# Six exps per head group on VectorE with GpSimd's square, and the next group's q and keys loaded head by head, in a graph-attention kernel

## The chip, the cores and the metric

The kernel runs on one core of a Trainium2 chip, in one launch. The time is device microseconds; 10982.1 us is the median of three runs of the kernel before (10978.02 to 10984.69). Profiles are of one further execution each. The engines are called as in the profile: PE (TensorE), ACT (ScalarE), DVE (VectorE), POOL (GpSimd) and SP (SyncE, which here only issues DMAs).

## The reference

Four graph layers act on x, 3327 nodes by 128 features, with one dense 3327 x 3327 matrix `adj`. Each layer normalises x, applies its function and adds the result to x. The change concerns layer 0 alone, an attention with 128 heads of 8 elements, whose scores get `adj` added twice:

```python
q = (x @ Wq.T).reshape(d, n, h); k = ...; v = ...        # d = 128 heads, n = 3327, h = 8
a = jnp.einsum('dnh,dmh->dnm', q, k) * scale
a = a + spatial_encoding + edge_encoding                 # both are adj
a = jax.nn.softmax(a, axis=2)
out = jnp.einsum('dnm,dmh->dnh', a, v)
return out.reshape(n, h * d) @ Wo.T
```

So there are 128 x 3327 x 3327 exps. Layers 1 to 3 are multiplications with `adj` and hyperbolic maps; they take the last some 800 us and are not touched.

## The kernel before, in words

**Tiling.** Scores are made transposed, keys on the 128 partitions and queries along the free dimension. A *chunk* `c` is 476 queries (7 chunks), a *group* `g` is four heads (32 groups), and a *pair* `q` is two tiles of 128 keys (13 pairs, r = 0 and 1 for the two tiles). The loop runs over 7 x 32 x 13 = 2912 pairs `u`, chunk by chunk, group by group; there are 224 head groups. A pair owns two of seven PSUM banks of the tile `S`, one per key tile (`banks`, line 618), and keeps them for its four heads. When the two banks are neighbours, one ACT exp covers both (128 x 952); in one pair of seven they wrap around and take two exps of 128 x 476.

**One pair.** DVE *seeds* each bank with `adj` less a bound (`seed`, L645). PE adds head 0's scores; ACT takes exp(2 S) of the bank into the tile `e0` (`exps`, L666 for the double form, L669 for a single). For the next head PE adds the difference of the two heads' scores to the same bank (the tiles `QS` and `KT` hold the next q and the negated last one side by side), ACT takes the exp again into `e1`, and so on to `e3`. PE then multiplies the exps with the values, 9 columns per head, into the bank `po` (`values`, L713); at a group's last pair DVE copies `po` to `OS` (L721) and POOL issues four DMAs of it (L725).

**The exps by hand.** In the pairs of `BY_HAND` (0, 2, 5, 7 and 10 of each group, here called hand pairs) head 0's exp of the second key tile is not ACT's. Its bank starts without a seed; DVE reads the bare scores (L691, its result in `h`), seeds the bank, and evaluates a polynomial of degree four in three operations (L695) and one (L697) that also multiplies with `EA`, the exp of twice the seed, which `shifted` (L678) and `bare` (L683) make once per chunk and hand pair. So in a hand pair ACT's first exp is a single. Because the polynomial comes late, `heads_of` (L699) has PE take this exp into the values one turn later than the others.

**The order of the work is written out by hand.** One loop (line 796) runs over slots `i`, four per pair, each slot one ACT exp; a place such as "slot 2 of pair 3" means `i % 4 == 2` there. Head j of pair u has its exp in slot 4u + 3j, so heads of neighbouring pairs are interleaved. In each slot the instructions of every engine are issued in program order: the exp, the DVE steps of the polynomial (slot 0 of a hand pair: L691 and the bank's seed; slot 3: one operation; slot 0 of the next pair: two; its slot 3: the last), seeds in slot 1 (the next pair's second bank, unless that is a hand pair) and slot 2 (first bank of the pair after the next). In odd slots PE gets the scores of the next two slots and four heads' values of one tile. Engines run their queues in order and wait on semaphores.

**Loads.** `loads(u)`, at the end of slot 0, brings in the next group: at pair 1 all keys of its four heads (`load_k`, 16 DMAs of 104 or 208 KB), head 0's q (`load_q`, 6 DMAs, 9 for head 1) and the values `VR`; at pairs 3, 5 and 7 POOL writes the negated q of one head into `QS` (`negate_q`, L570) and SP loads the next head's q; at pair 8 POOL spreads the values into `VA` (L580) and copies one column of the keys into `seen` (`all_here`, L584), for which the next group's first scores wait. All of these go through SP's queue in program order. In some groups DVE also transposes squares of `adj` for the next chunk (L288).

Of the kernel before, what the change touches and what calls it, by code (L numbers as in the profile page):

```python
# [10 lines left out]
F32 = mybir.dt.float32  # L11
# [6 lines left out]
ALU = mybir.AluOpType  # L18
# [4 lines left out]
P = 128  # L23
N = 3327
D = 128
H = 8
# [3 lines left out]
NQ = NT // 2  # L30
# [6 lines left out]
CW = 476  # L37
# [8 lines left out]
NOTHING = -1.0e30  # L46


EXP_C = (0.9999990463256836, 2.2162604331970215, 2.4563632011413574, 1.8291265964508057)
EXP_ARG = 0.9023826718330383  # L50
BY_HAND = (0, 2, 5, 7, 10)
LN_EPS = 1e-5
L1_EPS = 1e-7
L1_MAX_TANH = 1.0 - 1e-6
# [34 lines left out]
def gnn_kernel(ctx: ExitStack, tc: tile.TileContext, x, adj, Wq, Wk, Wv, Wo, embed, layer,  # L89
               embed_bias, layer_bias, weight, bias, W_in, W_out, out):  # L90
    nc = tc.nc
# [14 lines left out]
    kS_d = dram.tile([2, H, HEADS, NP], F32, name="kS_d")  # L106
# [418 lines left out]
    with tc.tile_pool(name="e1", bufs=1) as e1, tc.tile_pool(name="e_adj", bufs=28) as e_adj, \  # L525
# [12 lines left out]
        S = e_ps.tile([P, 7, 512], F32, name="S")  # L538
        po = e_ps.tile([P, 512], F32, name="po")

        def load_k(c, g):

            b = (c * NG + g) % 2
            for j in range(4):
                d = 4 * g + j
                k0, nk = max(0, j - 1), 1 if j in (0, 3) else 2
                for r in range(2):
                    r0 = 64 * r + 32 * (1 - j % 2)
                    k_d = kS_d[:, :, d, r * NQ * P:(r + 1) * NQ * P].rearrange("i e n -> (i e) n")
                    for i in range(2):  # L550
                        nc.sync.dma_start(KT[b][r0 + 16 * i:r0 + 16 * i + 16, k0:k0 + nk, :].bitcast(F32),
                                          k_d.unsqueeze(1).to_broadcast([16, nk, NQ * P]))

        def load_q(c, g, j):

            b = (c * NG + g) % 2
            w, c0, d = width_of(c), c * CW, 4 * g + j
            q_d = qS_d[:, :, d * N + c0:d * N + c0 + w].rearrange("i e n -> (i e) n")
            for r in range(2):
                r0 = 64 * r + 32 * (1 - j % 2)  # L560
                for q_s in [QS[b][:, j, :]] + [QZ[b]] * ((r, j) == (1, 1)):
                    nc.sync.dma_start(q_s[r0:r0 + 16, :w].bitcast(F32), q_d)
                    for i in range(2):
                        nc.sync.dma_start(q_s[r0 + 16 + 8 * i:r0 + 24 + 8 * i, :w].bitcast(F32),
                                          q_d[8 - 8 * i:16 - 8 * i])
# [33 lines left out]
        with tc.If(loose < 1), tc.manual_schedule():  # L599
# [28 lines left out]
            def touch(u, rows, x):  # L628
                of = {banks(u)[r] for r in rows}
                for y, other in touched:  # L630
                    if not of & other and x.ins.engine != y.ins.engine:
                        tc.declare_no_dep(x.ins, y.ins, reason="other banks")
                for i in of:
                    if i in last:
                        tc.add_manual_dep(x.ins, last[i].ins.name, after, reason="the same bank")
                    last[i] = x
                touched.append((x, of))

            def bank(u, r):
                return S[:, banks(u)[r], :width_of(pairs[u][0])]  # L640
# [19 lines left out]

            def exps(u, j):
                w, (even, odd) = width_of(pairs[u][0]), banks(u)
                e = e_of[u, j] = e_e.tile([P, 2, CW], F32, name=f"e{j}", bufs=(5, 4, 3, 2)[j])
                hand = j == 0 and by_hand(u)
                if even > odd and not hand:
                    touch(u, (0, 1), nc.scalar.activation(e[:, :, :w], S[:, odd:even + 1, :w], AF.Exp, scale=2.0))  # L666
                    return
                for r in range(1 if hand else 2):
                    touch(u, [r], nc.scalar.activation(e[:, 1 - r, :w], bank(u, r), AF.Exp, scale=2.0))  # L669

            def by_hand(u):

                return 0 <= u < n and pairs[u][2] in BY_HAND

            def shifted(c, q):

                w = width_of(c)
                nc.vector.tensor_tensor(EA[q][:, :w], adj_of[c][2 * q + 1][:, :w], shift_of[c][:, :w], op=ALU.subtract)  # L678

            def bare(c, q):  # L680

# [3 lines left out]
            def hand_exp(u):  # L685


                w = width_of(pairs[u][0])
                s = e_h.tile([P, CW], F32, name="h")[:, :w]
                e = e_of[u, 0][:, 0, :w]  # L690
                touch(u, [1], nc.vector.tensor_scalar(s, bank(u, 1), EXP_ARG, None, op0=ALU.mult))  # L691
                seed(u, 1)
                yield
                for k in (3, 2, 1):
                    nc.vector.scalar_tensor_tensor(e, s if k == 3 else e, EXP_C[k], s, op0=ALU.add, op1=ALU.mult)  # L695
                    yield
                nc.vector.scalar_tensor_tensor(e, e, EXP_C[0], EA[pairs[u][2]][:, :w], op0=ALU.add, op1=ALU.mult)  # L697

            def heads_of(u, r):  # L699


                first = (u, r)
                if by_hand(u) and r == 1:
                    first = (u + 1, 0)
                elif by_hand(u - 1):
                    first = (u, 1) if r == 0 else (u - 1, 1)
                return [first] + [(u, r)] * 3

            def values(u, r):
                c, g, q = pairs[u]  # L710
                w, k = width_of(c), c * NG + g
                for j, (v, of) in enumerate(heads_of(u, r)):
                    nc.tensor.matmul(po[32 * j:32 * j + H + 1, :w], VA[k % 2][:, 2 * pairs[v][2] + of, j, :],  # L713
                                     e_of[v, j][:, 1 - of, :w], start=(q == 0 and r == 0),
                                     stop=(q == NQ - 1 and r == 1))

            def store(u):
# [9 lines left out]
            def loads(u):  # L727

                c, g, q = pairs[u]
                k = c * NG + g  # L730
                if k + 1 < NC * NG:
                    nxt = divmod(k + 1, NG)
                    if q == 1:
                        load_k(*nxt)
                        load_q(*nxt, 0)
                        v_of[k + 1] = load_v(*nxt)
                    if q in (3, 5, 7):
                        negate_q(*nxt, q // 2 - 1)
                        load_q(*nxt, q // 2)
                    if q == 8:  # L740
                        spread_v(*nxt, v_of.pop(k + 1))
                        here[k + 1] = all_here(*nxt)
                if c + 1 < NC and (g, q) == (0, 0):
                    plan_squares(c)
                if g == NG - 1 and c + 1 < NC:
                    if q == 0:
                        shift_of[c + 1] = load_shift(c + 1)
                        adj_of[c + 1] = []
                    while len(adj_of[c + 1]) < min(NT, 2 * q + 6):
                        adj_of[c + 1].append(load_adj(c + 1, len(adj_of[c + 1])))  # L750
# [17 lines left out]
                        plan(u + k, f)  # L768

            v0 = load_v(0, 0)  # L770
            load_k(0, 0)
            load_q(0, 0, 0)
            shift_of[0] = load_shift(0)
            for j in range(3):
                negate_q(0, 0, j)
# [20 lines left out]
            for i in range(-4, 4 * n + 15):  # L796
                u, j = in_slot(i)
                if 0 <= u < n:
                    exps(u, j)
                at = i % 4  # L800
                if i == -4:
                    seed(0, 0)
                if at == 0 and by_hand(i // 4):
                    by_vector.append(hand_exp(i // 4))
                    next(by_vector[-1])
                for k in range(0 if at % 3 else 1 if at else 0 if by_hand(i // 4) else 2):
                    if by_vector and next(by_vector[0], True):
                        by_vector.popleft()
                if at == 0 and i >= 0:
                    for f, a in behind.pop(i // 4, ()):  # L810
                        f(*a)
                if at == 1 and (i + 3) // 4 < n and not by_hand((i + 3) // 4):
                    seed((i + 3) // 4, 1)
                u = (i - 14) // 4
                if at == 2 and 0 <= u < n and pairs[u][2] == NQ - 1:
                    store(u)
                if at == 2 and (i + 6) // 4 < n:
                    seed((i + 6) // 4, 0)
                if at % 2:
                    for k in (1, 2):  # L820
                        u, j = in_slot(i + k)
                        if 0 <= u < n:
                            scores(u, j)
                    u, r = ((i - 11) // 4, 0) if at == 3 else ((i - 13) // 4, 1)
                    if 0 <= u < n:
                        values(u, r)
                if at == 0 and 0 <= i // 4 < n:
                    loads(i // 4)
# [678 lines left out]
```

## Time and profile before

| What | Value |
| --- | --- |
| Median of three runs | 10982.1 us |
| The profiled execution | 10981.96 us |
| Its span, first to last instruction | 10980.2 us |
| First and last exp of the attention loop (L666, L669) | 462.5 and 10167.6 us |
| Busy from 4000 to 6000 us: PE, ACT, DVE, POOL | 1982.40, 1995.56, 1606.90, 270.68 us |
| Granted TensorE clock from 1000 to 10000 us | 1.00 |
| DMA: share of 16 engines, rate from 4000 to 6000 us | 0.59, 97 GB/s |
| Instructions per whole run: L666, L669 | 9024, 4128 |
| L691, L695 (first of three), L695 (other two), L697 | 1120, 1120, 2240, 1120 |
| L645 (seeds), mean | 5824, 676 ns |

How to read the profile: a row of a timeline is the start (us), the time from the first start to the last end of the merged instructions, the engine, the line, output and inputs by tile names, shapes, a count, and in brackets the idle time before it and what ended it. A row of the groups has the count, then the busy time in all (us) and the mean of one (ns), then the engine's idle time before. Instructions of one engine overlap by their pipelines, so the step from start to start is what one costs in a full queue, and a mean duration is longer than that. An instruction that holds its engine while it waits counts as busy.

### The profile page before, as it was taken

To read this page: it belongs to the slowest core of one execution; us is meant where nothing else is said; L and a number is where in the kernel's file an instruction comes from. 1 tells how busy PE (TensorE), PEld (TensorE's weight loads), DVE (VectorE), ACT (ScalarE), POOL (GpSimd) and SP (SyncE) were. 2 spreads that over 40 slices of the span, in tenths; PEclk is the share of its full clock that TensorE was granted. 3 is DMA by queue.
4 is the path that set the end of the run, shared out by engine and by line. 5 is a ranking of instruction groups with operands and counts; after the bars stand their busy time and mean duration, and the time that the engine had idled before them with its cause. 6 is when DMAs were issued, how large, how long until landed. Compare 5 with 4: busy or idle time off the path is not lost. (4 is left out here: it accounts for less than half of the span.)

```text
span 10980.2 us, 204474 instructions
## 1 busy us (share of the span) xinstructions
PE 10533.5 (96%) x72876; PEld 3435.7 (31%) x72876; DVE 8487.1 (77%) x13503; ACT 10033.1 (91%) x13789; POOL 1529.1 (14%) x2477
## 2 busy tenths in 40 slices
PE   4599999999999999999999999999999999999889
PEld 2133333333333333333333333333323333333544
DVE  5588887888878887788887888878877777777655
ACT  3599999999999999999999999999999999999330
POOL 5011111111111111111111111111111111111101
PEclk7799999999999999999999999999999999999999
DMA  8766566565566565565556565565556555554668
GB/s 250 250 99 97 94 96 113 93 98 96 89 118 97 93 97 88 106 98 97 90 95 119 94 96 93 95 119 95 87 93 98 96 95 86 82 88 71 206 233 281
DMA packets 695339, 1256.98 MB, mean 114 GB/s; under 512 B 195218, under 2 KB 555049, under 8 KB 691244
## 3 DMA queue, kind: packets, MB, share of 16 engines
q1 hardware_dynamic: 644044, 1114.42, 55.7%
q0 software_dynamic: 50272, 129.37, 4.3%
q8 instruction: 587, 9.62, 0.4%
q14 instruction: 436, 3.57, 0.2%
HBM read 1096.53 MB, written 146.60 MB: 113 GB/s over the span
## 5 line engine op out<-in xcount | busy, mean ns | idle before, releaser
L666 ACT ACTIVATE e<-S 128x952 f32<-128x952 f32 (+1 forms) x9024 | 8357.9, 1099 | 36.7 <-PE S L654 29.4
L713 PE MATMUL po<-e,VA 128*9 128x476 f32 (+1 forms) x46592 | 5737.5, 564 | 33.0 <-DVE OS L721 12.3
L645 DVE TENSOR_TENSOR S<-a,shb 128x476 f32<-128x476 f32 (+1 forms) x5824 | 3937.9, 676 | 1447.6 <-ACT e L666 1059.4
L654 PE MATMUL S<-QS,KT 64*128 64x476 f32 (+1 forms) x22176 | 4528.6, 445 | 79.7 <-DMA a<-adjT 28.4
L654 PEld LDWEIGHTS S<-QS,KT 64*128 64x128 f32 x22176 | 2073.7, 184 | 5100.5 <-issue 1301.3
L669 ACT ACTIVATE e<-S 128x476 f32<-128x476 f32 (+1 forms) x4128 | 2467.5, 711 | 1.1 <-PE S L654 0.6
L695 DVE SCALAR_TENSOR_TENSOR e<-e,h 128x476 f32<-128x476 f32 (+1 forms) x2240 | 1497.8, 669 | 77.0
L713 PEld LDWEIGHTS po<-e,VA 128*9 128x9 f32 x46592 | 691.0, 88 | 1606.6 <-issue 1488.1
L570 POOL TENSOR_SCALAR QS<-QS 128x476 fp32r<-128x476 f32 (+1 forms) x672 | 485.6, 723 | 4312.1 <-DMA QS<-qS_d 2612.2
L725 POOL DMA_DIRECT2D oT_d<-OS x896 | 470.5, 530 | 3668.8 <-DVE OS L721 3625.5
L691 DVE TENSOR_SCALAR h<-S 128x476 f32<-128x476 f32 (+1 forms) x1120 | 728.0, 650 | 300.9 <-PE S L654 296.5
L697 DVE SCALAR_TENSOR_TENSOR e<-e,EA 128x476 f32<-128x476 f32 (+1 forms) x1120 | 759.6, 678 | 0.0
L695 DVE SCALAR_TENSOR_TENSOR e<-h 128x476 f32<-128x476 f32 (+1 forms) x1120 | 743.1, 663 | 0.0
L1107 PE MATMUL pu<-strip,y 128*128 128x512 f32 (+2 forms) x1456 | 600.5, 566 | 31.7 <-DVE y L968 14.8
L654 PE MATMUL S<-QZ,KT 64*128 64x476 f32 (+1 forms) x1120 | 493.4, 441 | 11.9 <-DVE S L645 10.5
L1107 PEld LDWEIGHTS pu<-strip,y 128*128 128x128 f32 (+1 forms) x1456 | 271.9, 191 | 305.8 <-issue 272.1
L1111 DVE TENSOR_REDUCE deg<-strip 128x1 f32<-128x1536 f32 (+1 forms) x104 | 193.8, 1881 | 63.7 <-DMA strip<-adjT 44.1
L580 POOL COPY VA<-VR 128x832 f32<-128x832 f32 x224 | 242.3, 1082 | 0.0
L654 PEld LDWEIGHTS S<-QZ,KT 64*128 64x128 f32 x1120 | 205.1, 183 | 92.2 <-DVE S L645 52.4
L288 DVE STREAM_TRANSPOSE cols<-rows 128x416 f32<-128x416 f32 x208 | 204.5, 988 | 30.3 <-DMA rows<-in_adj_dram 22.6
L1060 ACT COPY uT<-pu 128x512 f32<-128x512 f32 (+1 forms) x21 | 11.1, 555 | 222.6 <-PE pu L1107 222.6
L721 DVE COPY OS<-po 128x476 f32<-128x476 f32 (+1 forms) x224 | 146.3, 653 | 87.3 <-PE po L713 87.3
(255 smaller groups left out, 1958.6 us busy)
## 6 DMA issues: line engine op xcount, KB each, us to landing
KT<-kS_d SPq DMA_DIRECT2D x1792, 208.0 KB
KT<-kS_d SPq DMA_DIRECT2D x1792, 104.0 KB
VR<-v_d SPq DMA_DIRECT2D x224, 416.0 KB
QS<-qS_d SPq DMA_DIRECT2D x3072, 14.9 KB
QS<-qS_d SPq DMA_DIRECT2D x1536, 29.8 KB
adjT<-cols SPq DMA_DIRECT2D x26, 1664.0 KB
a<-adjT SPq DMA_DIRECT2D x156, 238.0 KB
strip<-adjT POOLq DMA_DIRECT2D x39, 895.5 KB, 5.1
```

The costliest lines, as they stand in the source:

```text
L570: nc.gpsimd.tensor_scalar(QS[b][:, j + 1, :w], QS[b][:, j, :w].bitcast(F32), -1.0, 0.0, op0=ALU.mult, op1=ALU.add)
L580: nc.gpsimd.tensor_copy(VA[(c * NG + g) % 2][:, :, :, 0:H], v.rearrange("p j (t e) -> p t j e", e=H))
L645: touch(u, [r], nc.vector.tensor_tensor(bank(u, r), adj_of[c][2 * q + r][:, :w], shift_of[c][:, :w], op=ALU.subtract))
L654: x = nc.tensor.matmul(bank(u, r), KT[b][64 * r:64 * r + 64, max(0, j - 1), q * P:(q + 1) * P], q_s[64 * r:64 * r + 64, :w], start=hand an ...
L666: touch(u, (0, 1), nc.scalar.activation(e[:, :, :w], S[:, odd:even + 1, :w], AF.Exp, scale=2.0))
L669: touch(u, [r], nc.scalar.activation(e[:, 1 - r, :w], bank(u, r), AF.Exp, scale=2.0))
L691: touch(u, [1], nc.vector.tensor_scalar(s, bank(u, 1), EXP_ARG, None, op0=ALU.mult))
L695: nc.vector.scalar_tensor_tensor(e, s if k == 3 else e, EXP_C[k], s, op0=ALU.add, op1=ALU.mult)
L697: nc.vector.scalar_tensor_tensor(e, e, EXP_C[0], EA[pairs[u][2]][:, :w], op0=ALU.add, op1=ALU.mult)
L713: nc.tensor.matmul(po[32 * j:32 * j + H + 1, :w], VA[k % 2][:, 2 * pairs[v][2] + of, j, :], e_of[v, j][:, 1 - of, :w], start=(q == 0 and r ...
L725: nc.gpsimd.dma_start(oT_d[:, d * N + c * CW:d * N + c * CW + w], o[32 * j:32 * j + H + 1, :w])
L1107: nc.tensor.matmul(ps[:, :k], y[:m, t, :], s[:m, c * 4 * P - c0:c * 4 * P - c0 + k], start=(t == 0), stop=(t == NT - 1))
```

## The change

1. `BY_HAND` is (0, 2, 4, 6, 8, 10): six exps per group by hand instead of five, always two pairs apart.
2. The polynomial of degree four is evaluated in another form: z = s + C0 (L691's place), z squared **by POOL**, then three DVE operations instead of four: z = (e + C1) + z with the square in e, e = (e + C2) * z, e = (e + C3) * EA. The leading factor goes into EA through `EXP_LEAD`.
3. The steps are moved: slot 0 of a hand pair has z, POOL's square and the seed; slot 0 of the next pair the first two of the three; its slot 3 the last operation. Slot 3 of a hand pair has none.
4. The values take all four heads in the same order everywhere (`heads_of` is gone), and `e0` has four buffers instead of five.
5. The next group's loads: at pairs 1, 3, 5 and 7 one head's q and then that head's keys; the values at pair 1; spreading and `all_here` at pair 9 instead of 8. The number and size of DMAs stay.

```diff
-BY_HAND = (0, 2, 5, 7, 10)
+BY_HAND = (0, 2, 4, 6, 8, 10)
...
-        def load_k(c, g):
+        def load_k(c, g, j):
...
-                e = e_of[u, j] = e_e.tile([P, 2, CW], F32, name=f"e{j}", bufs=(5, 4, 3, 2)[j])
+                e = e_of[u, j] = e_e.tile([P, 2, CW], F32, name=f"e{j}", bufs=(4, 4, 3, 2)[j])
...
-                nc.vector.tensor_tensor(EA[q][:, :w], adj_of[c][2 * q + 1][:, :w], shift_of[c][:, :w], op=ALU.subtract)
+                nc.vector.scalar_tensor_tensor(EA[q][:, :w], adj_of[c][2 * q + 1][:, :w], EXP_LEAD, shift_of[c][:, :w],
+                                               op0=ALU.add, op1=ALU.subtract)
...
-                s = e_h.tile([P, CW], F32, name="h")[:, :w]
+                v, add, mult = nc.vector.scalar_tensor_tensor, ALU.add, ALU.mult
+                z = e_h.tile([P, CW], F32, name="h")[:, :w]
                 e = e_of[u, 0][:, 0, :w]
-                touch(u, [1], nc.vector.tensor_scalar(s, bank(u, 1), EXP_ARG, None, op0=ALU.mult))
+                touch(u, [1], nc.vector.tensor_scalar(z, bank(u, 1), EXP_C[0], None, op0=add))
+                nc.gpsimd.tensor_tensor(e, z, z, op=mult)
                 seed(u, 1)
                 yield
-                for k in (3, 2, 1):
-                    nc.vector.scalar_tensor_tensor(e, s if k == 3 else e, EXP_C[k], s, op0=ALU.add, op1=ALU.mult)
-                    yield
-                nc.vector.scalar_tensor_tensor(e, e, EXP_C[0], EA[pairs[u][2]][:, :w], op0=ALU.add, op1=ALU.mult)
...
+                v(z, e, EXP_C[1], z, op0=add, op1=add)
+                yield
+                v(e, e, EXP_C[2], z, op0=add, op1=mult)
+                yield
+                v(e, e, EXP_C[3], EA[pairs[u][2]][:, :w], op0=add, op1=mult)
...
-                for j, (v, of) in enumerate(heads_of(u, r)):
-                    nc.tensor.matmul(po[32 * j:32 * j + H + 1, :w], VA[k % 2][:, 2 * pairs[v][2] + of, j, :],
-                                     e_of[v, j][:, 1 - of, :w], start=(q == 0 and r == 0),
+                for j in range(4):
+                    nc.tensor.matmul(po[32 * j:32 * j + H + 1, :w], VA[k % 2][:, 2 * q + r, j, :],
+                                     e_of[u, j][:, 1 - r, :w], start=(q == 0 and r == 0),
...
-                    if q == 1:
-                        load_k(*nxt)
-                        load_q(*nxt, 0)
-                        v_of[k + 1] = load_v(*nxt)
                     if q in (3, 5, 7):
                         negate_q(*nxt, q // 2 - 1)
+                    if q in (1, 3, 5, 7):
                         load_q(*nxt, q // 2)
-                    if q == 8:
+                        load_k(*nxt, q // 2)
+                    if q == 1:
+                        v_of[k + 1] = load_v(*nxt)
+                    if q == 9:
                         spread_v(*nxt, v_of.pop(k + 1))
...
-                for k in range(0 if at % 3 else 1 if at else 0 if by_hand(i // 4) else 2):
+                for k in range(0 if at % 3 or by_hand(i // 4) else 1 if at else 2):
```

More of the change, by code (lines that the diff above doesn't have):

```diff
@@ L46 @@
 NOTHING = -1.0e30
-EXP_C = (0.9999990463256836, 2.2162604331970215, 2.4563632011413574, 1.8291265964508057)
-EXP_ARG = 0.9023826718330383
-BY_HAND = (0, 2, 5, 7, 10)
+EXP_C = (0.25674915313720703, 0.05050157010555267, 1.8002841472625732, 0.8117094039916992)
+EXP_LEAD = -0.2054332047700882
+BY_HAND = (0, 2, 4, 6, 8, 10)
 LN_EPS = 1e-5
@@ L539, in gnn_kernel @@
         po = e_ps.tile([P, 512], F32, name="po")
-        def load_k(c, g):
+        def load_k(c, g, j):
             b = (c * NG + g) % 2
[L544 to L552, printed above, removed]
+            d = 4 * g + j
+            k0, nk = max(0, j - 1), 1 if j in (0, 3) else 2
+            for r in range(2):
+                r0 = 64 * r + 32 * (1 - j % 2)
+                k_d = kS_d[:, :, d, r * NQ * P:(r + 1) * NQ * P].rearrange("i e n -> (i e) n")
+                for i in range(2):
+                    nc.sync.dma_start(KT[b][r0 + 16 * i:r0 + 16 * i + 16, k0:k0 + nk, :].bitcast(F32),
+                                      k_d.unsqueeze(1).to_broadcast([16, nk, NQ * P]))
         def load_q(c, g, j):
@@ L688, in hand_exp @@
                 w = width_of(pairs[u][0])
-                s = e_h.tile([P, CW], F32, name="h")[:, :w]
+                v, add, mult = nc.vector.scalar_tensor_tensor, ALU.add, ALU.mult
+                z = e_h.tile([P, CW], F32, name="h")[:, :w]
                 e = e_of[u, 0][:, 0, :w]
-                touch(u, [1], nc.vector.tensor_scalar(s, bank(u, 1), EXP_ARG, None, op0=ALU.mult))
+                touch(u, [1], nc.vector.tensor_scalar(z, bank(u, 1), EXP_C[0], None, op0=add))
+                nc.gpsimd.tensor_tensor(e, z, z, op=mult)
                 seed(u, 1)
                 yield
-                for k in (3, 2, 1):
-                    nc.vector.scalar_tensor_tensor(e, s if k == 3 else e, EXP_C[k], s, op0=ALU.add, op1=ALU.mult)
-                    yield
-                nc.vector.scalar_tensor_tensor(e, e, EXP_C[0], EA[pairs[u][2]][:, :w], op0=ALU.add, op1=ALU.mult)
[L699 to L707, printed above, removed]
+                v(z, e, EXP_C[1], z, op0=add, op1=add)
[3 more added lines that the diff above has]
+                v(e, e, EXP_C[3], EA[pairs[u][2]][:, :w], op0=add, op1=mult)
             def values(u, r):
@@ L770, in gnn_kernel @@
             v0 = load_v(0, 0)
-            load_k(0, 0)
             load_q(0, 0, 0)
+            for j in range(4):
+                load_k(0, 0, j)
             shift_of[0] = load_shift(0)
```

## The prediction

> **What bounds the kernel now.** I read the profiled execution first: 10981.96 us, of which the span is 10980.2 and 1.76 lie around it; the median of the runs is 10982.1, the same within 0.002%, so I add differences to 10982. The page's busy times and costliest groups come first, then the windows view.
>
> ```profile
> span 10980.2 us, 204474 instructions
> PE 10533.5 (96%) x72876; PEld 3435.7 (31%) x72876; DVE 8487.1 (77%) x13503; ACT 10033.1 (91%) x13789; POOL 1529.1 (14%) x2477
> ...
> L666 ACT ACTIVATE e<-S 128x952 f32<-128x952 f32 (+1 forms) x9024 | 8357.9, 1099 | 36.7 <-PE S L654 29.4
> ...
> L669 ACT ACTIVATE e<-S 128x476 f32<-128x476 f32 (+1 forms) x4128 | 2467.5, 711 | 1.1 <-PE S L654 0.6
> ```
> ```profile
> core 0: us, PE busy (x) PEld busy (x) DVE busy (x) ACT busy (x) POOL busy (x), PEclk, DMA share, GB/s
> ...
> 4000.00:6000.00 2000.00, 1982.40 (x14416) 606.16 (x14414) 1606.90 (x2473) 1995.56 (x2720) 270.68 (x433) 1.00 0.59 97
> ```
>
> In the attention loop ACT is busy 1996 us of 2000, DVE 1607, POOL 271; PE shows 1982, but its matmuls overlap. So I look at what one exp takes, start to start, in ACT's timeline.
>
> ```profile
> 5004.38 6.20 ACT L666 ACTIVATE e<-S 128x952 f32<-128x952 f32 x7
> 5010.30 1.21 ACT L669 ACTIVATE e<-S 128x476 f32<-128x476 f32 x2
> 5011.19 2.03 ACT L666 ACTIVATE e<-S 128x952 f32<-128x952 f32 x2
> ```
>
> Seven double exps take 5.92 us (0.846 each), two singles 0.89 (0.445). Over the loop the medians are 0.844 and 0.447. 9024 x 0.844 + 4128 x 0.447 + 35 x 0.45 for EA = 9477 us; the loop's exps run from 461 to 10168, 9707 us. So ACT loses 230 us between exps: 1.03 us per head group (224 groups of 43.3 us, 13 pairs of 3.33). The busy share hides it: an exp that is waited for shows as a long one.
>
> Where, from the start times of all groups: 0.31 at pair 4, 0.10 at pair 8, 0.05 at 11 (behind DVE's backlog), and 0.08 to 0.16 in the two pairs from a hand pair on that has no backlog (0, 5, 10; mean 0.12). The backlog: pairs 2 and 3 hold ten DVE operations of 0.65 to 0.69 us, in 6.7 us.
>
> ```profile
> 5456.77 1.34 DVE L695 SCALAR_TENSOR_TENSOR e<-e,h 128x476 f32<-128x476 f32 x2
> ...
> 5458.02 1.42 DVE L645 TENSOR_TENSOR S<-a,shb 128x476 f32<-128x476 f32 x2
> ...
> 5458.12 1.31 PE L654 MATMUL S<-QS,KT 64*128 64x476 f32 x4
> ```
>
> The seed follows the polynomial, and PE's four matmuls take 1.31 instead of 0.70. The other kind is PE's own: a round of four score matmuls and eight of values takes 1.55 us (5482.26 to 5483.81), a hand pair's first two exps 0.45 + 0.84 = 1.29.
>
> **The change, part by part.**
>
> *One more exp off ACT.* 224 pairs more lose one exp. Banks wrap in one pair of seven: 192 doubles become singles, 32 wrapped pairs lose a single: -192 x 0.844 + 160 x 0.447 = -90.5. One more EA per chunk: 7 x 0.45 = +3. **ACT: -87 us.**
>
> *DVE.* 6 x 4 operations instead of 5 x 5: 0.67 us less per group, with DVE at 80%: nothing by itself. (EA's subtraction becomes a form with a constant, 0.65 us like L697, seven more in all: nothing.) But with hand pairs two apart and two hand operations moved from slot 3 to the next pair, pairs 0 to 10 have four operations each (2.7 of 3.3 us), 11 has five. The 0.46 us of backlog stalls go; what is late next is the seed below. The hand exps are ready some five slots (4 us) before their values matmul, so dropping the swapped order and the fifth e0 buffer costs nothing; without that cover, a slot (0.84 us) each.
>
> *GpSimd's square, the disputed cost.* No POOL product of this width is in the trace; the nearest rows are of the first stage:
>
> ```profile
> L369 POOL TENSOR_TENSOR sq<-sq 128x512 f32<-128x512 f32 x47 | 59.6, 1268 | 25.5 <-ACT sq L367 24.5
> L369 POOL TENSOR_TENSOR sq<-sq 128x256 f32<-128x256 f32 x47 | 33.9, 722 | 3.8
> ```
>
> A line through these gives 1.19 us at 476 columns. The new wait, of the first add for the square, comes a pair (3.3 us) after z; behind it on DVE stand the next hand operation and a seed that PE needs five slots later, so it costs nothing while POOL is not blocked. On POOL the square waits for z; behind it are the store's DMAs and the negations, for which nobody hurries. But see DVE beside POOL:
>
> ```profile
> 5478.90 0.65 DVE L691 TENSOR_SCALAR h<-S 128x476 f32<-128x476 f32 x1 [0.66 <-PE S L654]
> 5479.59 0.66 DVE L645 TENSOR_TENSOR S<-a,shb 128x476 f32<-128x476 f32 x1
> ...
> 5480.66 1.43 DVE L645 TENSOR_TENSOR S<-a,shb 128x476 f32<-128x476 f32 x2 [0.42 <-ACT e L666]
> ...
> 5481.62 0.70 PE L654 MATMUL S<-QS,KT 64*128 64x476 f32 x4
> ...
> 5482.44 0.66 POOL L570 TENSOR_SCALAR QS<-QS 128x476 fp32r<-128x476 f32 x1 [3.62 <-PE S L654]
> ...
> 5482.68 2.17 DVE L695 SCALAR_TENSOR_TENSOR e<-e,h 128x476 f32<-128x476 f32 x2
> ...
> 5483.05 1.31 POOL L580 COPY VA<-VR 128x832 f32<-128x832 f32 x1
> ```
>
> Two operations that take 1.34 above take 2.17 here: the first ends 0.50 after the negation, the second 0.49 after the copy. So a DVE operation with two SBUF inputs waits until a POOL operation has ended. The other way round, a negation (0.58 alone) that meets such an operation ends 0.44 after it, so 0.14 of it is start-up. L691, which reads PSUM, was never longer beside POOL.
>
> Now pair 10 as the example of a hand pair. z ends 5479.55; the seed of its own bank starts at once, ends 5480.25. POOL, released some 0.3 after z (as the OS copy and its DMA show), waits for that seed and then holds DVE out for 1.19 - 0.14 = 1.05, to 5481.30. The next pair's seed, ready at 5480.66, ends 5481.81 instead of 5481.33; PE, ready at 5481.62, waits 0.24. Over all hand pairs, adding this to their own starts gives PE 0.20 and ACT, after its slack, 0.11 (0.04 at pair 0, 0.17 at 5). The trace has the same by nature: at pair 10, 27 seeds were lengthened by POOL; the five that ended 2.55 to 2.65 us into the pair (the change would put it at 2.60 to 2.69) lost 0.26 in the two pairs, the 190 untouched 0.157: 0.10 more; at pair 0, five seeds that ended at 2.6 to 2.9 lost 0.46 against 0.143: 0.32. The lower end is 0 (all in PE's slack), the upper 0.30; **I take 0.13**, close to the first two readings and a little above them for the third. Then stalls are 6 x (0.12 + 0.13) + 0.15 for pair 12 and the chunk edges = 1.65 per group, against 1.03: 0.62 x 224 = **+139 us**.
>
> The Trainium skill, "SBUF — State Buffer", section "Who interferes with whom", speaks against the change: whichever of a GpSimd operation and a two-SBUF-input VectorE operation issues first keeps the shared pair to its end. The rows agree that it is exclusive. A neighbouring section measured the loser resuming 115 ns after; with the seed's whole 0.66 that would be 0.27 later than the rows' 0.51, an estimate of up to 0.27 x 1344 = 363 us more. The rows decide.
>
> *Loads.* The same DMAs, in another order; SP issues them at 0.3 us each and is on no path. Today the first negation waits until pair 8 behind sixteen key transfers; then POOL must be free for squares. Head 0's q now goes ahead of its keys, so negation 0 runs at about 3.8 pairs, after the 2.1 us of store DMAs. Negations follow a q load by 4.1 us (its idle before the row at 5478.23), and 832 KB of keys take 5.3 us (161 GB/s at a DMA share of 1.00 from 5454 to 5470). So negations at 5.1 and 7.1 pairs, keys complete at 10.0, all_here done at 10.2, and the square of pair 10 behind it at 10.6, needed at 11.0. Nothing, with 1.2 us to spare.
>
> **Sum:** 10982 - 87 + 139 = 11034, say **11033**. Break-even is at 0.09 per hand pair, so it is a close call.
>
> **Rivals.**
> *Faster: the blocked seed fits into PE's slack.* In pair 10 PE could take it until 5481.57, so it costs nothing if POOL holds DVE out for under 0.81 us after the seed, not 1.05. Then stalls are 6 x 0.12 + 0.15 = 0.87, 0.16 less than now: 10982 - 36 - 87 = 10859. For it: the smoother DVE, and ACT's 0.04 at pair 0. Against: the rows of 722 and 1268 ns.
> *Slower still: POOL's queue.* If all_here ends a pair late, pair 10's square, and DVE behind it, wait up to 3.3 us; about 1.4 remain after the seeds' slack and pair 12: 224 x 1.4 = +314, 11350. For: 1.2 us of margin. Against: pair 12 has one DVE operation.
> *No change:* ACT's gain is eaten to the last, at 0.09 per hand pair: 10982.
>
> **How the numbers follow.** Forecast, a loss of 0.05 to 0.30 per hand pair: 60%; at 13.4 us per 0.01, its own range is 10926 to 11261. Faster rival 22%, queue 11%, no change 7%. The range 10850 to 11250 leaves out a third of the faster rival, nearly all of the queue and the forecast's edge: 2 in 10. 0.2% (22 us) is about what a measurement can tell from no change. Of the forecast, 0.44 lies above 11004, 0.07 within 22 us, 0.09 below; with the rivals: slower 0.55, same 0.14, faster 0.31.
>
> **What would show it.** POOL's squares of about 1.19 to 1.8 us, six per group; L645's mean well above 676 ns, with the long ones just after a square; no loss at pair 4, losses of 0.2 to 0.3 at each of 0 to 10; 8832 doubles, 4288 singles. DVE idle on POOL at the first add would mean the queue rival; seeds of 0.66 beside squares would mean that I read the lock wrongly, and the faster rival.

## The result, and the profile after

The changed kernel takes 11408.7 us (11397.97 to 11412.79, four runs) against 10982.5: a ratio of 1.0387, 95% interval 1.0369 to 1.0405. The forecast was 11033 with a range to 11250: the sign was right, the size was far too small, and the time lies outside, next to the rival that I gave 11% (POOL's queue, 11350).

The page after; the columns are those of the page before.

```profile
span 11407.3 us, 207811 instructions
PE 10624.7 (93%) x72876; PEld 3404.3 (30%) x72876; DVE 8826.6 (77%) x13286; ACT 10009.4 (88%) x13764; POOL 3222.4 (28%) x3821
...
L665 ACT ACTIVATE e<-S 128x952 f32<-128x952 f32 (+1 forms) x8832 | 8127.1, 1039 | 423.0 <-PE S L653 408.6
L644 DVE TENSOR_TENSOR S<-a,shb 128x476 f32<-128x476 f32 (+1 forms) x5824 | 4313.9, 741 | 1110.5 <-ACT e L665 774.7
...
L693 POOL TENSOR_TENSOR e<-h 128x476 f32<-128x476 f32 (+1 forms) x1344 | 1719.2, 1279 | 3611.5 <-DVE h L692 3363.7
L668 ACT ACTIVATE e<-S 128x476 f32<-128x476 f32 (+1 forms) x4288 | 2434.6, 652 | 67.7 <-PE S L653 66.5
L696 DVE SCALAR_TENSOR_TENSOR h<-e,h 128x476 f32<-128x476 f32 (+1 forms) x1344 | 997.0, 742 | 583.8 <-POOL e L693 583.8
...
L583 POOL COPY seen<-KT 128x3 f32<-128x3 f32 x224 | 46.5, 208 | 1597.7 <-DMA KT<-kS_d 1555.6
```

ACT now shows idle time, 423 us before its double exps, and nearly all of it (409) waits for PE. Two other rows say where that begins: L696, the first add of the polynomial, had DVE idle for 584 us until the square was there (the prediction's own sign of the queue rival), and on POOL the copy to `seen` sat idle for 1556 us until keys had landed. The squares (L693) stand in the same queue as that copy. The window of the middle of the loop has ACT at 1909 us of 2000, where it had 1996:

```profile
core 0: us, PE busy (x) PEld busy (x) DVE busy (x) ACT busy (x) POOL busy (x), PEclk, DMA share, GB/s
...
4000.00:6000.00 2000.00, 1920.18 (x13830) 575.15 (x13827) 1610.62 (x2334) 1908.92 (x2602) 592.79 (x683) 0.98 0.52 91
```

One group's POOL timeline, then DVE's, around pairs 8 to 12, and last the rows of PE and ACT in which the wait ends:

```profile
5704.25 0.59 POOL L569 TENSOR_SCALAR QS<-QS 128x476 fp32r<-128x476 f32 x1 [7.97 <-DMA QS<-qS_d]
5704.81 0.98 POOL L693 TENSOR_TENSOR e<-h 128x476 f32<-128x476 f32 x1
5705.73 0.88 POOL L579 COPY VA<-VR 128x832 f32<-128x832 f32 x1
5718.54 0.19 POOL L583 COPY seen<-KT 128x3 f32<-128x3 f32 x1 [11.93 <-DMA KT<-kS_d]
5718.68 0.98 POOL L693 TENSOR_TENSOR e<-h 128x476 f32<-128x476 f32 x1
```
```profile
5708.85 0.65 DVE L692 TENSOR_SCALAR h<-S 128x476 f32<-128x476 f32 x1
5709.53 2.19 DVE L644 TENSOR_TENSOR S<-a,shb 128x476 f32<-128x476 f32 x3
5719.69 0.65 DVE L696 SCALAR_TENSOR_TENSOR h<-e,h 128x476 f32<-128x476 f32 x1 [7.97 <-POOL e L693]
...
5720.95 1.42 DVE L644 TENSOR_TENSOR S<-a,shb 128x476 f32<-128x476 f32 x2
```
```profile
5721.66 1.16 PE L653 MATMUL S<-QS,KT 64*128 64x476 f32 x3 [6.54 <-DVE S L644]
5722.46 1.82 ACT L665 ACTIVATE e<-S 128x952 f32<-128x952 f32 x2 [6.75 <-PE S L653]
```

The z of pair 10 is there at 5709.50. Its square could run at once; it runs at 5718.68, because `seen` stands before it and waits for keys. DVE's add waits with it, the next pair's seeds (5720.95) wait behind the add, PE's scores for the seeds (6.54 us), and ACT for PE (6.75 us).

**The sum by loss.** I took each exp's start and counted what exceeds 0.844 us (double) or 0.447 us (single). Before, ACT lost 229 us, 1.02 per group; after, 746 us, 3.33 per group. The difference, 517, less the 87 us that the exps save (90, less 3 for seven more exps of EA), is 430; the two profiled executions differ by 11409.3 - 10982.0 = 427. So the change of time is in those losses, to within 3 us. By pair (us per group, mean of 224):

| Pair | 0 | 1 | 2 | 3 | 4 | 5 | 6 | 7 | 8 | 9 | 10 | 11 | 12 |
| --- | --- | --- | --- | --- | --- | --- | --- | --- | --- | --- | --- | --- | --- |
| before | 0.14 | 0.00 | 0.14 | 0.01 | 0.35 | 0.04 | 0.03 | 0.01 | 0.11 | 0.02 | 0.07 | 0.06 | 0.04 |
| after | 0.17 | 0.03 | 0.15 | 0.01 | 0.09 | 0.51 | 0.01 | 0.02 | 0.02 | 0.22 | 0.30 | 0.43 | 1.38 |

Pairs 9 to 12 have 2.33 of the 3.33, and pair 5 has 0.51.

### The profile page after: what moved, and what is told of

Same layout as the page of the kernel before. It is cut to its first block, busy times and chain, and to the rows that moved or that the text cites. A ratio compares the mean times of both kernels' runs of the same rounds, so it can differ in the third digit from the quotient of the medians.

```text
span 11407.3 us, 207811 instructions
## 1 busy us (share of the span) xinstructions
PE 10624.7 (93%) x72876; PEld 3404.3 (30%) x72876; DVE 8826.6 (77%) x13286; ACT 10009.4 (88%) x13764; POOL 3222.4 (28%) x3821
## 5 line engine op out<-in xcount | busy, mean ns | idle before, releaser
L665 ACT ACTIVATE e<-S 128x952 f32<-128x952 f32 (+1 forms) x8832 | 8127.1, 1039 | 423.0 <-PE S L653 408.6
L644 DVE TENSOR_TENSOR S<-a,shb 128x476 f32<-128x476 f32 (+1 forms) x5824 | 4313.9, 741 | 1110.5 <-ACT e L665 774.7
L653 PE MATMUL S<-QS,KT 64*128 64x476 f32 (+1 forms) x21952 | 4394.1, 441 | 299.9 <-DVE S L644 261.3
L653 PEld LDWEIGHTS S<-QS,KT 64*128 64x128 f32 x21952 | 1996.2, 186 | 5199.6 <-issue 1673.6
L693 POOL TENSOR_TENSOR e<-h 128x476 f32<-128x476 f32 (+1 forms) x1344 | 1719.2, 1279 | 3611.5 <-DVE h L692 3363.7
L696 DVE SCALAR_TENSOR_TENSOR h<-e,h 128x476 f32<-128x476 f32 (+1 forms) x1344 | 997.0, 742 | 583.8 <-POOL e L693 583.8
L692 DVE TENSOR_SCALAR h<-S 128x476 f32<-128x476 f32 (+1 forms) x1344 | 872.7, 649 | 209.6 <-PE S L653 198.9
L700 DVE SCALAR_TENSOR_TENSOR e<-e,EA 128x476 f32<-128x476 f32 (+1 forms) x1344 | 978.9, 728 | 0.0
L698 DVE SCALAR_TENSOR_TENSOR e<-e,h 128x476 f32<-128x476 f32 (+1 forms) x1344 | 889.0, 661 | 46.2
L653 PE MATMUL S<-QZ,KT 64*128 64x476 f32 (+1 forms) x1344 | 619.1, 461 | 128.9 <-DVE S L644 108.8
```

What stands on the lines that cost most here:

```text
L644: touch(u, [r], nc.vector.tensor_tensor(bank(u, r), adj_of[c][2 * q + r][:, :w], shift_of[c][:, :w], op=ALU.subtract))
L653: x = nc.tensor.matmul(bank(u, r), KT[b][64 * r:64 * r + 64, max(0, j - 1), q * P:(q + 1) * P], q_s[64 * r:64 * r + 64, :w], start=hand an ...
L692: touch(u, [1], nc.vector.tensor_scalar(z, bank(u, 1), EXP_C[0], None, op0=add))
L693: nc.gpsimd.tensor_tensor(e, z, z, op=mult)
L696: v(z, e, EXP_C[1], z, op0=add, op1=add)
L698: v(e, e, EXP_C[2], z, op0=add, op1=mult)
```

## The experiments

Three theories went in. The **queue**: squares stand in POOL's queue behind waits for DMAs. The **lock**: a square shuts DVE's seeds out (my forecast). **Late keys**: the next group's first scores wait for keys whatever POOL does. Each experiment starts from the changed kernel unless it says otherwise.

**1. `all_here` behind the last square.**

```diff
-                    if q == 9:
+                    if q == 11:
                         spread_v(*nxt, v_of.pop(k + 1))
                         here[k + 1] = all_here(*nxt)
```

> The changed kernel with one step moved: the values are spread and all_here waits for the keys at pair 11 instead of 9, behind the square of pair 10. Three theories. Queue theory: the square of pair 10 stands in POOL's queue behind a wait for the keys' DMAs (DVE idle 2.4 us per group at that pair); then most of the 2.1 us per group that ACT loses at pairs 10 to 12 goes, down to about 0.4: 11409 - 1.7 x 224 = about 11030 (10980 to 11080). Lock theory (a square shuts DVE's seeds out): no change, 11400. Late-keys theory (the next group's first scores wait for the keys): no change or slower, 11400 and up.

11020.9 us, 1.0036 [1.0024, 1.0049] of before: 388 us back by one number. DVE's wait for squares falls from 584 to 54 us, and ACT's losses at pairs 10 to 12 from 2.1 to 0.33 us per group:

```profile
L696 DVE SCALAR_TENSOR_TENSOR h<-e,h 128x476 f32<-128x476 f32 (+1 forms) x1344 | 930.9, 693 | 53.9 <-POOL e L693 53.9
```

The queue theory's number was 11030. The lock and the late keys are out as main causes: a square still keeps DVE's seeds out for 0.83 us after the seed before it, as in the changed kernel, and the keys are known to be there no earlier (`all_here` ends at 11.4 pairs, in the changed kernel at 11.1; medians).

**2. Also the negation of head 2 behind the square of pair 8.**

```diff
-                    if q in (3, 5, 7):
-                        negate_q(*nxt, q // 2 - 1)
-                    if q in (1, 3, 5, 7):
-                        load_q(*nxt, q // 2)
-                        load_k(*nxt, q // 2)
+                    if q in (3, 5, 8):
+                        negate_q(*nxt, {3: 0, 5: 1, 8: 2}[q])
+                    if q in (1, 3, 5, 8):
+                        load_q(*nxt, {1: 0, 3: 1, 5: 2, 8: 3}[q])
+                        load_k(*nxt, {1: 0, 3: 1, 5: 2, 8: 3}[q])
```

> As the first, and head 2's negation with head 3's loads at pair 8 instead of 7, so behind the square of pair 8. Queue theory: that square no longer waits behind a negation that waits for q (48 us of DVE's idle time), and the 0.2 us per group lost at pair 9 mostly goes: 20 to 50 us below the first, 10950 to 11040. Lock theory: 11400. Late-keys theory: the keys come no earlier, 11400 or slower.

11128.6 us, 1.0134 [1.0117, 1.0151]: a miss, 108 us slower than the first. The wait that I meant did go (pair 9 loses 0.00 instead of 0.21), but pair 0 loses 0.93 instead of 0.17. Of that 0.63 is at its first exp, nearly all of it in 22 groups, 4 to 8 us each. They are those after a transposed square is stored: that store of 1664 KB is issued at pair 8 ahead of the loads, so it now went before head 3's keys in SP's queue.

**3. The store moved behind the keys** (pair 10 instead of 8, on top of the second).

```diff
-                    for k, f in ((0, sq.gather), (1, sq.back), (7, sq.finish), (8, sq.store)):
+                    for k, f in ((0, sq.gather), (1, sq.back), (7, sq.finish), (10, sq.store)):
```

> The second experiment (negation 2 and head 3's loads at pair 8, 11129 us) with the transposed square's store of 1664 KB planned at pair 10 instead of 8, so that in SP's queue it stands behind head 3's loads. If the 0.63 us per group at pair 0 and part of the 0.26 in its slot 2 came from the 22 groups in which that store went ahead of the keys, they go: 11129 - 0.75 x 224 = 10960 (10930 to 11000), now 20 to 70 us below the first experiment. If head 3's later loads are the cause in all groups: 11100 and more.

10973.5 us, 0.9994 [0.9984, 1.0003]: 155 us back, as that explanation asks, and no difference from before that can be measured. DVE's wait for squares is 2.6 us in all:

```profile
L696 DVE SCALAR_TENSOR_TENSOR h<-e,h 128x476 f32<-128x476 f32 (+1 forms) x1344 | 931.1, 693 | 2.6 <-POOL e L693 2.6
```

So the queue's waits are worth 11409 - 10974 = 435 us: all of the loss, and six hand exps without them are no gain either.

**4. The new loads alone**, in the kernel before (five exps without POOL, `load_k` and `loads` as changed).

> The kernel before with the new loads alone (five hand exps without POOL, loads head by head, spreading at pair 9). Queue theory: nothing urgent stands in POOL's queue, so 10960 to 11010, as before. Late-keys theory: the keys arrive at pair 11 and PE waits for them at the next group, so slower by 200 us or more, 11200. Lock theory: 10982.

11084.5 us, 1.0093 [1.0076, 1.011]: not free, though nothing on POOL is urgent there. The losses that grew are at pairs 4 (0.35 to 0.58), 9 (0.02 to 0.35) and 2 (0.14 to 0.23). Negation 0 now ends at 3.9 pairs, where it ended at 7.1, and the spreading at 8.7, where it ended at 10.2 (medians). In pairs 3 and 8 DVE is behind, and there these two now shut its seeds out: the seed of pair 4's second bank was longer than 0.72 us in 57% of groups (before: none), that of pair 9's in 57% (before: 8%). Beside every one of these long seeds the negation or the spreading was running. At these places PE needs no new keys, so I read this as the lock again, where it costs most; no experiment took these two operations away.

**5. The new exps alone**, with the loads as they were.

```diff
+                    if q == 1:
+                        for j in range(4):
+                            load_k(*nxt, j)
+                        load_q(*nxt, 0)
+                        v_of[k + 1] = load_v(*nxt)
                     if q in (3, 5, 7):
                         negate_q(*nxt, q // 2 - 1)
-                    if q in (1, 3, 5, 7):
                         load_q(*nxt, q // 2)
-                        load_k(*nxt, q // 2)
-                    if q == 1:
-                        v_of[k + 1] = load_v(*nxt)
-                    if q == 9:
+                    if q == 8:
```

> The changed kernel with the loads as they were (all keys at pair 1, spreading at pair 8). Queue theory: in the kernel before, negation 0 ended at 7.2 pairs, 1 at 8.5 and 2 at 9.9; squares 4 to 10 now stand behind them, DVE waits over two pairs at pair 5 alone: +5 us per group or more, 12000 to 13000. Lock theory: as the changed kernel, 11400. Late-keys theory: the keys come early again, so the exps show their gain, 10900 to 11000.

13028.9 us, 1.1865 [1.1842, 1.1889]. The queue theory named 12000 to 13000, just missed. One group of its POOL timeline shows the mechanism:

```profile
6009.47 2.12 POOL L718 DMA_DIRECT2D oT_d<-OS  x4 [1.64 <-DVE OS L714]
6022.93 0.58 POOL L569 TENSOR_SCALAR QS<-QS 128x476 fp32r<-128x476 f32 x1 [11.34 <-DMA QS<-qS_d]
6023.48 0.97 POOL L693 TENSOR_TENSOR e<-h 128x476 f32<-128x476 f32 x1
```

A square right behind a negation that waited 11.3 us for q; ACT loses 7.3 us per group at pair 6 and 2.4 at 7. So the reordered loads are what makes POOL's squares bearable at all, and the two halves of the change can't be judged one by one.

**6. What the lock costs at most: a fill instead of the square** (on top of the first; POOL reads nothing from SBUF, and the polynomial gets ones for the square).

```diff
-                nc.gpsimd.tensor_tensor(e, z, z, op=mult)
+                nc.gpsimd.memset(e, 1.0)
```

> The first experiment with the square replaced by a POOL fill of the same tile with ones, which reads no SBUF (the exp by hand is so computed from 1 instead of the square). Lock theory: no seed is shut out any more, so the means of the seeds fall from 0.74 to 0.67 us and the 0.49 us per group at pair 5 and what else the lock costs go: 11021 - 0.5 x 224 = 10910 or less. If it's DVE's count of operations at the OS copy alone: 11000 to 11030.

10971.6 us, 0.9991 [0.9981, 1.0001], 49 us less than the first, between the numbers of the two theories. The seeds' mean falls from 755 to 670 ns:

```profile
L644 DVE TENSOR_TENSOR S<-a,shb 128x476 f32<-128x476 f32 (+1 forms) x5824 | 3904.9, 670 | 1786.4 <-ACT e L665 1397.2 <-ACT e L668 164.6 <-DMA QS<-qS_d 2.9
L693 POOL MEMSET e<- 128x476 f32 (+1 forms) x1344 | 666.2, 496 | 3574.5 <-PE po L706 2241.8 <-ACT e L665 993.4 <-ACT e L668 332.4
```

The seeds are back at their length of 0.66, yet pair 5 still loses 0.47 of 0.51: that place belongs to DVE's own backlog. 49 us, 49 / 1344 = 0.036 per hand pair, is the upper end of what the lock costs the kernel with the square, since the fill changes more than the lock. It is shorter and doesn't wait for z, and DVE's wait for it falls from 54 to 26 us; pair 9 alone, where the square stood behind a negation, goes from 0.21 to 0.04 us per group, 38 us. The third experiment brought that place to 0.00 with the squares kept.

**7. A product of two tiles instead of the square of one** (on top of the first; the polynomial gets z times EA instead of the square).

```diff
-                nc.gpsimd.tensor_tensor(e, z, z, op=mult)
+                nc.gpsimd.tensor_tensor(e, z, EA[pairs[u][2]][:, :w], op=mult)
```

> The first experiment with POOL's product taken of z and EA instead of z and z (so the exp by hand is computed from that product, not from the square). The square alone took 0.98 us, a line through the first stage's products of two parts of a tile gave 1.19. If reading one tile twice is what saves it: 1.19 alone, 0.2 us longer hold of DVE's seeds, and by the lock theory up to 0.2 x 6 x 224 = 270 us slower, by the queue theory some 0.1 us per hand pair, 11100 to 11200. If the width or the product is the cause: 0.98 and 11021.

11135.1 us, 1.014 [1.0123, 1.0157], 114 us more than the first. The view of the line has minimum, median and maximum in ns; first the changed kernel's squares, then these products:

```profile
L693 POOL TENSOR_TENSOR e<-h x1344: 967/1376/1483, 460.6 to 10581.9; 128x476 f32<-128x476 f32 x165, 128x472 f32<-128x472 f32 x27
```
```profile
L693 POOL TENSOR_TENSOR e<-h,EA x1344: 1182/1607/1735, 459.9 to 10306.6; 128x476 f32<-128x476 f32 x165, 128x472 f32<-128x472 f32 x27
```

The minima are those that met no seed, the medians those that waited for one first. With two tiles the product takes 1.2 us and ends 1.06 after the seed before it; with one tile 0.97 and 0.83. My 1.19 and 1.05 were right for two tiles. At that length the lock costs at most 11135.1 - 10971.6 = 163.5 us (against the fill), 0.12 per hand pair, where I had taken 0.13. The 114 us are the surer number: DVE's wait for POOL is no longer than in the first experiment (36 us, there 54), so they are the price of holding the seeds out 0.23 us longer.

**8. Other hand pairs, the free pair before the OS copy.** Hand pairs 0, 3, 5, 7, 9, 11, and OS's DMAs issued behind the square of pair 3 (on top of the first).

```diff
-BY_HAND = (0, 2, 4, 6, 8, 10)
+BY_HAND = (0, 3, 5, 7, 9, 11)
...
-                    store(u)
+                    out_of = store(u)
...
+                u = (i - 17) // 4
+                if at == 1 and 0 <= u < n and pairs[u][2] == NQ - 1:
+                    send(*out_of)
```

> The first experiment (all_here at pair 11, 11021 us) with hand pairs 0, 3, 5, 7, 9 and 11, so that the two pairs without DVE's backlog are 1 and 2, where the OS copy falls, and with the four DMAs of OS issued one slot after the square of pair 3. In the first experiment ACT lost 1.60 us per group: 0.49 at pair 5 (DVE late from the OS copy, its next seed then shut out by the square), 0.19 at pair 9 and 0.17 at 11 (squares behind negation 2 and the spreading). Queue theory with the lock as a lesser term: these go, 0.5 to 0.8 is left, so 11021 - 0.8 to 1.1 x 224 = 10775 to 10840, faster than both kernels. Lock theory (each square costs its hand pair 0.13 or more): 6 x 0.25 + 0.15 stays, 11000 and more.

11114.3 us, 1.0121 [1.0104, 1.0138]: a miss. The OS copy must wait for PE's last values of the group, so the z of pair 3, which now follows it in DVE's queue, starts 0.7 us after ACT's exp (most others 0.3 before it), and pairs 3 and 4 lose 1.00 us per group.

**9. The free pair after the OS copy**: hand pairs 0, 2, 5, 7, 9, 11, pair 2's polynomial stepped later (on top of the first).

```diff
-                for k in range(0 if at % 3 or by_hand(i // 4) else 1 if at else 2):
+                for k in range(0 if at % 3 or by_hand(i // 4) or (at == 0 and i // 4 % NQ == 3) else 1 if at else 2):
```

> The first experiment (all_here at pair 11, 11021 us) with hand pairs 0, 2, 5, 7, 9 and 11, so that the one free pair follows the OS copy, and the polynomial of pair 2 stepped later: none at slot 0 of pair 3, one operation in its slot 3, the last two at slot 0 of pair 4. Theory: the 0.5 us per group at pair 5 come from DVE, which has the OS copy on top and starts pair 4's z 0.5 us late; squares and negations lengthen that. Then pairs 3 to 5 lose under 0.1 and 0.6 is left of 1.60: 11021 - 1.0 x 224 = 10800 (10780 to 10870), faster than both kernels. If the squares themselves cost 0.13 or more at each hand pair: 10950 and more.

10974.0 us, 0.9992 [0.9983, 1.0001]. The place was right and the sum was not: pairs 3 to 5 lose 0.11 instead of 0.62 (the first experiment), but pairs 0, 1 and 6 lose 0.83 instead of 0.19.

**10. Five hand pairs with the square** (0, 4, 6, 8, 10, on top of the third, which the expectation calls the seventh).

> The seventh experiment (10974 us) without hand pair 2: five hand pairs 0, 4, 6, 8 and 10 with POOL's square, so ACT does what it did before and the pairs around the OS copy have no polynomial. Theory: the losses at pairs 2 to 5 (0.21 + 0.10 + 0.52) go, 0.5 us per group of losses is left against 1.02 before, at the same ACT work: 10982 - 0.5 x 224 = 10870 (10840 to 10920). If the sixth exp is worth its 87 us and the losses are not from the OS copy: 11060.

10973.2 us, 0.9993 [0.9984, 1.0002]: a miss. Without hand pair 2 the losses at pairs 2, 3 and 5 fall from 0.74 to 0.11. But pairs 4, 6 and 8, which lost 0.13 together, lose 0.35, most of it in their slot 2, 0.09 to 0.13 each. I read that as PE's pace, its round of 1.55 us against a hand pair's 1.29: after a stop ACT is late and PE ahead, and this loss doesn't show; take the stop away and part of it comes back here. No run changed PE's round alone, so this is argued, not shown. In all, the losses fell by 81 us, and the exps that ACT does again cost 87.

**11 and 12. POOL's other operations moved** (on top of the ninth): negation 1 and head 2's loads at pair 4, and the values spread at pair 10 (eleventh) or 8 (twelfth), `all_here` at 11 in both.

```diff
-                    if q in (3, 5, 7):
+                    if q in (3, 4, 7):
...
-                    if q == 11:
+                    if q == 10:
                         spread_v(*nxt, v_of.pop(k + 1))
+                    if q == 11:
                         here[k + 1] = all_here(*nxt)
```

> The ninth experiment (10974 us) with the spreading of the values at pair 10 instead of 11 and negation 1 with head 2's loads at pair 4 instead of 5. In the ninth ACT lost 0.23 us per group at pair 1 (the spreading ended at 12.0 pairs and kept DVE from its seeds before pair 0's z) and 0.24 at pair 6 (negation 1 at 5.9, right behind the square of pair 5). Theory (POOL's operations cost where DVE is late, and nothing else): half of these or more goes, 10974 - 0.25 x 224 = 10918 (10880 to 10950). If these losses are PE's pace around hand pairs: 10960 to 10990.

> As the eleventh, with the spreading at pair 8, ahead of the square of pair 9 and behind negation 2, which ended at 8.6 pairs. Theory: 0.9 to 1.3 us of spreading delay that square to 9.4 or so, which is still before 10.0, but it meets the seeds of pair 9: between the ninth and the eleventh, 10900 to 10980. Queue theory: not above 11000, since the values come early with head 0's keys.

The eleventh takes 10922.5 us, 0.9946 [0.9932, 0.9959]: **54 us faster than the kernel before**, 486 us faster than the changed one, and the only version that beats both. Pairs 0 and 1 lose 0.30 instead of 0.59, as meant; the earlier negation gained nothing (pair 6 loses 0.30 instead of 0.24). The twelfth takes 10982.7, 1.0003 [0.9994, 1.0012], a little above its range: the spreading ahead of pair 9's square costs 0.45 at pair 10.

## Why the prediction was wrong

**The step that failed is the loads': "Nothing, with 1.2 us to spare."** I had negations ending at about 3.8, 5.1 and 7.1 pairs, keys complete at 10.0 and `all_here` at 10.2. The negations' medians after are 3.9, 5.2 and 8.4, and `all_here` ended at 11.1. The first two are right. From negation 1 to 2 I let the 4.1 us of a q load and the 5.3 us of the previous head's keys overlap into 2.0 pairs; they add up. In the group above, head 2's q was issued right behind the 832 KB of head 1's keys:

```profile
5693.52 1.72 SPq L550 DMA_DIRECT2D KT<-kS_d  x4
5695.34 0.36 SPq L561 DMA_DIRECT2D QS<-qS_d  x1
...
5697.43 1.90 SPq L563 DMA_DIRECT2D QS<-qS_d  x2
```

From the first of these q DMAs to the negation that waited for them (5704.25) it took 8.9 us. The median of all groups is 9.1, against 3.7 in the kernel before, where no keys stood ahead of them: 5.4 more, the 5.3 of the keys. So negation 2 came 3.3 pairs after negation 1 instead of 2.0, and `all_here` 0.9 of a pair late. The rival had the mechanism and the chain (`all_here` a pair late, pair 10's square, DVE, seeds), and its 314 us were near: the first experiment gave back 388, and the third, which also frees pair 8's square from the wait for head 2's q, brings it to 435. That its 11350 lies so near 11409 is in part luck: it had the waits 121 us too low, and the lock, which it shares with the forecast, at least 126 too high (below). I gave it 11% since the margin looked like a third of a pair, but a margin that is the sum of four estimated DMA landings deserved more. Its argument against, that pair 12 has one DVE operation, was no argument: the seeds that PE needs next stand behind the blocked add, not in free time.

**ACT, -87:** right; 8832 and 4288 exps, and the losses add up with it.

**DVE, "The 0.46 us of backlog stalls go":** half wrong. The losses at pair 4's first slot went from 0.31 to 0.00 us, but 0.49 came at pair 5's. I counted four operations for each of pairs 0 to 10 and forgot the OS copy in pair 2, which also waits for PE. With it pair 4's z starts 0.2 us after ACT's first exp instead of 0.3 before. The ninth and tenth experiments emptied that place by giving DVE a free pair there.

**The lock:** the mechanism was right and the size was mis-sized. The next seed ended 0.51 to 0.52 us after the square, as the rows before had it, and L644's mean rose to 741 ns. But the hold was 0.83 us instead of 1.05, since the square reads one tile, just above the 0.81 that my faster rival named as its limit; so it costs at most 0.036 us per hand pair instead of 0.13 (sixth experiment), 49 us instead of 175. With two tiles it would have been up to 0.12. The Trainium skill, "SBUF — State Buffer", section "A bandwidth-pool intuition that's wrong (but worth ruling out)", has GpSimd's DMA descriptor writes, held up by a DVE operation, go on some 115 ns after that operation's end. If a seed of 0.66 us started only so long after a square, it would by this estimate end 0.775 us after it; the rows, of two compute operations, say 0.51.

**"Losses of 0.2 to 0.3 at each of 0 to 10", "no loss at pair 4":** neither. Pairs 6 and 7 lose 0.03 together, pair 4 still 0.09, and 0.51 is at pair 5, which is no hand pair.

**"Nothing" for the loads also missed the lock:** the fourth experiment shows 102 us for the new order in the old kernel, and long seeds beside the negation and the spreading. I looked at what waits for a negation and not at what a negation shuts out.

What stays open: the eleventh kernel still loses 1.19 us per group, and how much of it is PE's pace and how much DVE's order wasn't separated. Part 4 of the change (the order of the values, one buffer less) is in every experiment but the fourth and wasn't tried by itself.

## What to carry to other kernels

When an urgent operation joins an in-order queue, list every wait that stands before it in that queue, with the landing time of the DMA behind it, measured with all traffic ahead of it; waits that cost nothing so far become stalls, and moving one such wait behind the last urgent operation gave back 388 of 426 us here. Where small loads share a queue with large ones, add their times, don't overlap them: here 3.7 us of q behind 5.3 us of keys took 9.1. And a loss removed from one place can return at another (ninth and tenth experiment), so a sum of local losses is an upper end of the gain.

## What the runs showed of the hardware

- A POOL product that reads the same tile twice took 0.97 us for 128x476 and one that reads two tiles 1.18 (minima of 1344 each). A seed that a square had kept waiting ended 0.51 to 0.52 us after it.
- A POOL fill (0.496 us, no reading) lengthened no DVE operation noticeably: the 867 last operations of a polynomial (L700, two SBUF inputs) that ran beside one had a median of 0.648 us, the others 0.652. Few seeds met a fill, since it comes before them; their mean was 670 ns, against 755 in the kernel with squares and 809 with two-tile products. The Trainium skill, "SBUF — State Buffer", section "Who interferes with whom", says that such a DVE operation contends with a GpSimd instruction that reads SBUF and not with one that only writes it; these rows agree.
- The mean granted TensorE clock of the profiled executions was 0.985 before, 0.971 after, 0.976 in the second experiment, 0.91 in the fifth, and 0.983 to 0.985 in all others. So it was lowest where PE had the longest stops. Whether the lower clock adds to the time wasn't tried.
